# A graph network on one core: 24 instead of 20 of 98 receiver blocks summed by gathered rows, with their products placed in both kinds of TensorE stretches

## The chip, the core and the metric

The kernel runs on one core of a Trainium2 chip. The metric is the device time of an execution in microseconds. The engines are TensorE (PE, with its weight loads as PEld), VectorE (DVE), ScalarE (ACT), GpSimd (POOL) and SyncE (SP); SP and ACT issue plain transfers, POOL issues those that gather rows by a list of indices.

## The reference, cut to what matters

There are 12500 nodes with 64 features and 212500 directed edges, sorted by receiver (`dst`). Three layers take, for each node, the mean of its neighbours' rows; the last part takes the mean of the edges' own features and runs a small MLP.

```python
def _sage_conv(x, src, dst, Wl, Wr, b, n_nodes):
    msgs = x[src]
    summed = segment_sum(msgs, dst, num_segments=n_nodes)
    cnt = segment_sum(ones, dst, num_segments=n_nodes)
    agg = summed / maximum(cnt, 1.0)[:, None]
    return agg @ Wl + x @ Wr + b
...
h = maximum(_layernorm(x), 0.0)
x = x + L0(h)             # three _sage_conv, relu after the first two
h = maximum(_layernorm(x), 0.0)
x = x + L1(h)             # scatter_mean of edge_attr_64 by receiver,
                          # concatenated with h; 128 -> 64 -> 64 -> 64
```

## The kernel before, in words

The nodes are cut into 98 blocks of 128 (NB). A layer's neighbour sums are made per block of receivers, in one of two ways.

**Dense.** For 78 of the blocks (those from GB = 20 on), taken four at a time as 20 dense groups (the last has two), layer 0 builds the matrix of edge counts between all senders and the four receiver blocks, as 8-bit numbers. It is the product of two one-hot lists: DVE writes the lists (`hots`, L790 to L792), TensorE multiplies them (`pb`, L809), ACT writes the result to the matrix `m` (L812), and SP stores it in DRAM as `mat`. Layers 1 and 2 load it from there as `t`. A layer's sums are then products with the layer's rows, which are stored as three bf16 parts whose sum is the f32 value. `Layer.group` runs them in two kinds of steps: a **whole** step (L392) multiplies two parts of a sender block, 128 columns of weights, with the 512 receivers of the group; a **half** step (L403) multiplies the third part, 64 columns of weights, and steps of even and odd blocks use the lower and the upper half of the array. A group has 98 whole and 98 half steps.

**By edge.** For the first 20 blocks (GB), the rows of the edges' senders are fetched by an indirect transfer of POOL (`got`, L461), 128 edges at a time, EK = 19 times per block. DVE writes the matching one-hot of receivers (`own`, L336), and one product per 128 edges (`pg`, L489: 128x128 weights, 192 columns) adds them up. Per layer that is 20 x 19 = 380 fetches and products. A ring of NGOT = 8 buffers holds the fetched rows; the fetch for product i + 8 is issued behind product i (`Layer.use`). Every four blocks, `sums` transposes the result (L507), and `turn` (L425) and `mix` (L436, L440) follow, as they do for a dense group.

**The order** is written by hand. `Weave` runs a group in four stretches: 56 whole steps (TURN), 56 half steps, 42 whole, 42 half. Other work is hung on positions: `wide` on a count of whole steps over the layer (w), `narrow` on the index of a half step. The products by edge hang on `wide`, spread evenly by `spread` and `spot`; pb work hangs on both, 40 pairs of a four-block group on wide positions and 12 on narrow ones, two pairs at a time. The order holds for TensorE, DVE, ACT and POOL in layer 0, for TensorE and POOL in layer 1, for TensorE in layer 2.

**Lists.** For each node group, `index` finds where its edges begin: it fetches a tile of `dst` (`ends`, two buffers), lets ACT count in it (`inside`), and fetches the edges of single nodes (`to`, `of`). For blocks by edge, `lists` then fetches the edges' receivers and senders (`l_to`, `l_of`, L567) with POOL's indirect transfers, 8 per four blocks in two lots at steps 108 and 120 of the group's work, and DVE makes `place` and `rows_of` of them at step 150 (`places`).

**The edges' own features** are summed in layer 2, for all 98 blocks: SP loads a start address into a register (L1028) and then a block's edges from there (`raw`, `e_to`); 19 products per block (`pe`, L1138) stand among whole steps.

Of the kernel before, what the change touches and what calls it, by code (L numbers as in the profile page):

```python
# [11 lines left out]
F32 = mybir.dt.float32  # L12
# [17 lines left out]
P = 128  # L30
D = 64
# [12 lines left out]
WD = 5  # L44
FAR = 1 << 23
EK = 19
GB = 20
H1 = 10
QE = 5

# [21 lines left out]
def in_order(  # L72
# [221 lines left out]
    class Weave:  # L294
# [2 lines left out]

        def __init__(self):
            self.w, self.seq, self.wides, self.narrows = 0, 0, [], []

        def wide(self, pos, fn):
            self.seq += 1
            heapq.heappush(self.wides, (pos, self.seq, fn))

        def narrow(self, pos, sub, fn):
            self.seq += 1
# [2 lines left out]
        def run(self, whole, half):  # L309


            half = enumerate(half)
            for n in (TURN, None):
                for _ in islice(whole, n):
                    self.w += 1
                    while self.wides and self.wides[0][0] <= self.w:
                        heapq.heappop(self.wides)[2]()
                for i, _ in islice(half, n):
                    due = [f for f in self.narrows if f[0] <= i and f[1] <= self.w]
                    for f in sorted(due):  # L320
                        self.narrows.remove(f)
                        f[3]()
                    heapq.heapify(self.narrows)

        def rest(self):
            while self.wides or self.narrows:
                while self.narrows:
                    heapq.heappop(self.narrows)[3]()
                if self.wides:
                    heapq.heappop(self.wides)[2]()  # L330
# [13 lines left out]
    HALVES = ((0, H1), (H1, EK))  # L344
    CUTS = [(k, min(k + QE, EK)) for k in range(0, EK, QE)]
    NC = len(CUTS)
    NGOT = 8

    psd = ctx.enter_context(tc.tile_pool(name="ps_dense", bufs=1, space=PSUM))
    psc = ctx.enter_context(tc.tile_pool(name="ps_conv", bufs=1, space=PSUM))  # L350
# [5 lines left out]
    class Layer:  # L356
# [18 lines left out]
        def hand_over(self, to):  # L375

            w = self.weave
            for pos, _, f in sorted(w.wides, key=lambda a: a[:2]):
                to.weave.wide(pos - w.w, f)
            for sub, pos, _, f in sorted(w.narrows, key=lambda a: a[:3]):  # L380
                to.weave.narrow(pos - w.w, sub, f)
            self.weave, self.gap = to.weave, 0
# [96 lines left out]
        def use(self, i):  # L479
# [20 lines left out]
            if b % 4 == 3:  # L500
# [14 lines left out]
                w.narrow(w.w + 1, 40, sums)  # L515
                w.narrow(w.w + 1, 68, own_rows)

    steps = NB * len(dense_groups)

    def spot(i, first):  # L520
# [2 lines left out]

    def spread(layer, first):
        for i in range(EK * GB):
            layer.weave.wide(spot(i, first), lambda i=i: layer.use(i))


    TW = 4 * P
# [14 lines left out]
    with ExitStack() as s:  # L544
# [27 lines left out]
        def index(j, box):  # L572


            n0 = node0[:, j : j + 1]
            at = begins[:, j : j + 1]
            own = 32 * min(4, NB - 4 * j)
            tile = lambda name, n, dtype=F32, bufs=2: idx.tile([P, n], dtype, name=name, bufs=bufs)

            def over(t, bias, n, dtype, name, to):  # L580

                nc.scalar.activation(
                    tile(name, TW, dtype, 1)[:, :n], t, AF.Sign, bias=bias, scale=1.0, accum_out=to
                )

            def tiles():
                box["s"] = tile("tile_s", 1)
                over(heads, before[:, j : j + 1], TT, I8, "signs", box["s"])

            def ends():  # L590

                box["tile"] = tile("tile_of", 1)
                nc.vector.tensor_scalar(
                    box["tile"], box["s"], -0.5, 1.0 - TT / 2, op0=ALU.mult, op1=ALU.max
                )
                tile_i = tile("tile_i", 1, I32)
                nc.vector.tensor_scalar(tile_i, box["tile"], TT / 2 - 1.0, None, op0=ALU.add)
                box["ends"] = tile("ends", TW, I32)
                gather(box["ends"], tiles_d, tile_i[:, :1])

            def inside():
                box["in"] = tile("in_tile", 1)
                over(box["ends"], before[:, j : j + 1], TW, I8, "signs", box["in"])

            def edges():
                s = box["in"]
                nc.vector.tensor_scalar(
                    s, s, -0.5, TW / 2 + TW * (TT / 2 - 1.0), op0=ALU.mult, op1=ALU.add
                )
                nc.vector.scalar_tensor_tensor(  # L610
                    at, box["tile"], float(TW), s, op0=ALU.mult, op1=ALU.add
                )
                at_i = tile("at_i", 1, I32)
                nc.vector.tensor_scalar(at_i, at, float(EP - P), None, op0=ALU.min)
                box["to"], box["of"] = tile("to", P, I32), tile("of", P, I32)
                gather(box["to"], dst, at_i[:, :1])
                gather(box["of"], src, at_i[:, :1])

            def places():

                box["pos"], box["code"] = tile("pos", P), tile("code", P)
                pos, code = box["pos"], box["code"]
                nc.vector.tensor_scalar(pos, box["to"], n0, 7.0, op0=ALU.subtract, op1=ALU.min)
                nc.vector.scalar_tensor_tensor(
                    code, pos, float(1 << 14), box["of"], op0=ALU.mult, op1=ALU.add
                )
                behind = tile("junk", P, bufs=1)
                nc.vector.scalar_tensor_tensor(
                    behind, pos, size[:, :1], far, op0=ALU.is_ge, op1=ALU.mult
                )  # L630
                nc.vector.tensor_tensor(code, code, behind, op=ALU.max)

            def counts(d):
                if d == 0:
                    box["have"] = tile("have", WD + 1)
                over(
                    box["pos"], halves[:, d : d + 1], P, I8, "signs", box["have"][:, d : d + 1]
                )

            def alike():  # L640
                code = box["code"]
                for k in range(1, 5):
                    nc.vector.scalar_tensor_tensor(
                        tile("junk", P, bufs=1)[:own, k:], code[:own, k:], 0.0,
                        code[:own, : P - k], op0=ALU.add, op1=ALU.is_equal,
                        accum_out=twins[:own, j, k - 1 : k],
                    )
                have = tile("twice", WD)
                nc.vector.tensor_tensor(
                    have, box["have"][:, :WD], box["have"][:, 1:], op=ALU.subtract  # L650
                )
                box["by4"] = idx.tile([P, WD, 4], BF16, name="by4", bufs=2)
                nc.vector.tensor_tensor(
                    box["by4"], have[:, :, None].to_broadcast([P, WD, 4]),
                    mask4[:, None, :].to_broadcast([P, WD, 4]), op=ALU.mult,
                )
                box["first"] = tile("first", 4)
                nc.vector.tensor_scalar(box["first"], start4, at, None, op0=ALU.mult)

            return (  # L660
                [(0, tiles), (7, ends), (29, inside), (36, edges), (64, places)]
                + [(74 + 2 * d, lambda d=d: counts(d)) for d in range(WD + 1)]
                + [(91, alike)]
            )
# [67 lines left out]
        def lists(j):  # L732
# [3 lines left out]
            def edges(k0):  # L736
                if k0 == 0:
                    box["of"] = idx.tile([P, 4, EK], I32, name="l_of")
                    box["to"] = idx.tile([P, 4, EK], I32, name="l_to")
                for k in (k0, k0 + 1):  # L740
                    b = 4 * j + k
                    gather(box["to"][:, k, :], dst, mine[:, b : b + 1])
                    gather(box["of"][:, k, :], src, mine[:, b : b + 1])

            def places():
                for k in range(4):
# [273 lines left out]
    def load(b):  # L1020
        if b is None:
            return

        n = EK * P
        raw = ed.tile([P, n // P * D + 1], F32, name="raw")
        first = raw[:1, n // P * D :].bitcast(I32)
        nc.vector.tensor_scalar(first, mine[:1, b : b + 1], float(EP - n), None, op0=ALU.min)
        at0 = nc.values_load(  # L1028
            first, engines=[SP], min_val=0, max_val=EP - n,
            skip_runtime_bounds_check_because="it is clamped, and is not under 0",  # L1030
        )
        raw = raw[:, : n // P * D].rearrange("p (k d) -> p k d", d=D)
        nc.sync.dma_start(raw, edge[ds(at0, n), :].rearrange("(p k) d -> p k d", k=EK))
        if b < GB:
            box[b] = raw, place[:, b]
            return
        to = ed.tile([P, EK], I32, name="e_to")
        nc.sync.dma_start(to, dst[ds(at0, n), :].rearrange("(p k) o -> p (k o)", k=EK))
        at = ed.tile([P, EK, 2], BF16, name="e_at")
        nc.vector.tensor_scalar(  # L1040
            at, to[:, :, None].to_broadcast([P, EK, 2]), float(b * P), None, op0=ALU.subtract
# [736 lines left out]
```

## Time and profile before

| what | value |
|---|---|
| time, median of 3 runs | 2892.62 us (2887.84 to 2893.87) |
| the profiled execution | 2895.6 us, of which the span is 2893.7 |
| granted TensorE clock, mean | 0.985 |
| layer 0 with its preparation, about | 0 to 1130 us |
| layer 1, about | 1130 to 1876 us |
| layer 2 and the MLP, about | 1876 to 2894 us |
| TensorE busy in 160 to 1130, 1130 to 1876, 1876 to 2894 us | 948, 735, 997 us |
| POOL busy in the same stretches | 576, 363, 425 us |
| whole steps L392, halves L403, products by edge L489 | 5880, 5880, 1140 |

A line of the timeline gives the start and the length in us from the span's start, the engine (PE is a matmul), the line in the code, what is written and read, the tile of the array (128*64 is half of its columns), the shape and the count of merged instructions. Matmuls overlap, so the cost of one is read from the start of one row to the start of the next on the same engine, not from its length. A line of the waits gives who waited for whom, the total in us, the number of times and the longest. In the rows a matmul's outputs p1 and p2 are both called `p`.

### The profile page before, as it was taken

The numbers are of one execution on the slowest core, as the hardware profiler recorded it, in microseconds if no ns is written. First come the engines' busy times: TensorE is split into PE (matmuls) and PEld (weight loads), VectorE is DVE, ScalarE is ACT, GpSimd is POOL, SyncE is SP. The second block draws the span as 40 slices with busy tenths as digits, with TensorE's granted clock in tenths as the row PEclk, the third lists the DMA queues.
The fourth block names the chain that finished last, engine by engine and source line by source line (L and its number), as shares of the span: only waits on it lengthen the run. The fifth ranks groups of instructions, "written<-read, shape, count | busy, mean of one in ns | idle before, by whom it ended". The sixth has DMA issues, their size and how long they took to land.

```text
span 2893.7 us, 50078 instructions
## 1 busy us (share of the span) xinstructions
PE 2749.0 (95%) x19505; PEld 1600.9 (55%) x19505; DVE 1630.9 (56%) x3376; ACT 1122.5 (39%) x2339; POOL 1429.8 (49%) x1313
## 2 busy tenths in 40 slices
PE   1699999999999998999999999999999999999997
PEld 0455555555555554555555555655656565565655
DVE  8878788788788771211111111166666566666663
ACT  4666566666666661100000000033333333434332
POOL 5345667667575640555555555244444344444440
PEclk9999999999999998999999999999999999999998
DMA  3334434444444346766656665577667676667661
GB/s 97 160 128 169 154 137 169 169 164 149 160 167 156 138 158 224 236 212 210 208 190 205 210 212 191 191 232 238 218 200 226 195 231 216 203 219 232 207 211 36
DMA packets 203194, 537.43 MB, mean 186 GB/s; under 512 B 83874, under 2 KB 92195, under 8 KB 197955
## 3 DMA queue, kind: packets, MB, share of 16 engines
q1 hardware_dynamic: 143890, 458.08, 44.2%
q0 software_dynamic: 41360, 66.33, 10.2%
q10 hardware_dynamic: 17696, 9.74, 1.1%
q8 instruction: 154, 2.52, 0.4%
q14 instruction: 94, 0.76, 0.1%
HBM read 391.11 MB, written 142.90 MB: 185 GB/s over the span
## 4 chain that ended last, share of the span: by engine, by line
PE 83%; DVE 12%; DMA 3%; issue 1%; ACT 1%; POOL 0%; SPq 0%; ACTq 0%; DVEq 0%; POOLq 0%
PE p L392 39%; PE p L403 21%; PE pb L809 6%; PE pe L1138 5%; PE pg L489 3%; DVE c L792 3%; PE po L436 3%; PE po L440 3%; DVE h L790 2%; PE pt L425 2%; DVE h L791 1%; PE pm L1177 1%; PE pm L1186 1%; DMA ends<-in_dst_dram,tile_i 1%; DMA e_to<-in_dst_dram 1%
## 5 line engine op out<-in xcount | busy, mean ns | idle before, releaser
L461 POOL DMA_INDIRECT got<-h_d,rows_of x1140 | 1244.2, 1091 | 1246.0 <-PE pg L489 881.0
L812 ACT CAST m<-pb 128x490 uint16<-128x490 f32 (+1 forms) x1014 | 545.7, 564 | 329.1 <-PE pb L809 318.4
L392 PE MATMUL p<-m,rows 128*128 128x512 fp8e3 (+1 forms) x1960 | 569.6, 378 | 0.8 <-ACT m L812 0.8
L392 PEld LDWEIGHTS <-rows 128*128 128x128 bf16 x3920 | 374.6, 100 | 245.6 <-issue 45.9
L392 PE MATMUL p<-t,rows 128*128 128x512 fp8e3 (+1 forms) x1960 | 491.8, 378 | 0.9 <-ACT rows L263 0.9
L392 PE MATMUL p<-t,m 128*128 128x512 fp8e3 (+1 forms) x1960 | 458.4, 376 | 0.0
L809 PE MATMUL pb<-c,h 128*128 128x245 bf16 x2028 | 371.2, 276 | 57.0 <-ACT m L812 42.0
L336 DVE TENSOR_TENSOR own<-iota_l,place 128x640 bf16<-128x640 bf16 (+3 forms) x280 | 144.2, 516 | 360.2 <-PE pg L489 337.0
L403 PEld LDWEIGHTS <-rows 128*64 128x64 bf16 x3920 | 224.9, 110 | 217.5 <-issue 79.1
L809 PEld LDWEIGHTS <-h 128*128 128x128 bf16 x2028 | 190.9, 99 | 263.4 <-issue 105.5
L792 DVE TENSOR_TENSOR c<-iota_c,col 128x1968 bf16<-128x1968 bf16 (+1 forms) x234 | 298.6, 1276 | 0.0
L489 PE MATMUL pg<-got,own 128*128 128x192 bf16 x1140 | 281.7, 247 | 15.7 <-DVE ga L496 8.3
L392 PEld LDWEIGHTS <-m 128*128 128x128 bf16 x1960 | 184.7, 99 | 184.0 <-issue 13.9
L403 PE MATMUL p<-m,rows 128*64 128x512 fp8e3 (+1 forms) x1960 | 254.1, 378 | 0.0
L403 PE MATMUL p<-t,rows 128*64 128x512 fp8e3 (+1 forms) x1960 | 252.0, 377 | 0.0
L1052 ACT CAST cut<-raw 128x640 bf16<-128x640 f32 x196 | 136.5, 697 | 247.7 <-PE pe L1138 221.6
L790 DVE TENSOR_TENSOR h<-iota_l,lo 128x1024 bf16<-128x1024 bf16 (+1 forms) x234 | 173.6, 742 | 94.9 <-PE pb L809 94.4
L403 PE MATMUL p<-t,m 128*64 128x512 fp8e3 (+1 forms) x1960 | 225.5, 375 | 0.0
L1054 ACT CAST cut<-e_rest 128x640 bf16<-128x640 f32 x196 | 136.8, 698 | 221.5 <-DVE e_rest L1053 220.5
L1055 DVE TENSOR_TENSOR cut<-e_rest,cut 128x640 bf16<-128x640 f32 x196 | 154.8, 790 | 81.9 <-ACT cut L1054 81.4
L1138 PE MATMUL pe<-cut,own 128*128 128x192 bf16 x1862 | 188.3, 248 | 0.0
L1138 PEld LDWEIGHTS <-own 128*128 128x128 bf16 x1862 | 161.6, 99 | 40.5 <-issue 2.9
(189 smaller groups left out, 2566.1 us busy)
## 6 DMA issues: line engine op xcount, KB each, us to landing
t<-mat SPq DMA_DIRECT2D x546, 448.0 KB, 5.9
mat<-m SPq DMA_DIRECT2D x39, 3136.0 KB, 9.9
raw<-in_edge_dram SPq DMA_DIRECT2D x98, 608.0 KB, 4.1
got<-h_d,rows_of POOLq DMA_INDIRECT x1140
h_d<-rows SPq DMA_DIRECT2D x14, 336.0 KB, 2.2
h_d<-rows ACTq DMA_DIRECT2D x24, 192.0 KB, 2.5
h_d<-out SPq DMA_DIRECT2D x21, 192.0 KB, 1.9
m<-h_d SPq DMA_DIRECT2D x6, 576.0 KB
```

What stands on the lines that cost most here:

```text
L336: nc.vector.tensor_tensor(t[:, :n].rearrange("p k (c t) -> p k c t", t=2), iota_l.rearrange("p (c t) -> p c t", t=2)[:, None].to_broadcast ...
L392: nc.tensor.matmul(p1, rows[:, i, : 2 * D], at(i), start=i == 0, stop=i == NB - 1)
L403: nc.tensor.matmul(p2[h], rows[:, i, 2 * D :], at(i), start=i < 2, stop=i >= NB - 2)
L461: nc.gpsimd.indirect_dma_start(out=t, out_offset=None, in_=h_rows[self.l], in_offset=bass.IndirectOffsetOnAxis(ap=rows_of[:, b, k : k + 1] ...
L489: nc.tensor.matmul(self.pg[:, b % 2, :], self.owned.pop(i), self.fetched.pop(i), start=k == 0, stop=k == EK - 1,)
L790: nc.vector.tensor_tensor(split(th), pairs(iota_l, P), own(lo, P), op=ALU.is_equal)
L792: nc.vector.tensor_tensor(split(tc_), pairs(iota_c, CW), own(col, CW), op=ALU.is_equal)
L809: nc.tensor.matmul(pb[:, i, : HP * WD], h, c, start=True, stop=True)
L812: nc.scalar.copy(m[:, block // 2, :, o : o + 2 * k].rearrange("p h (w d) -> p h w d", d=k), pb[:, :, : HP * WD].rearrange("p w (h d) -> p ...
L1054: nc.scalar.copy(c[:, :, D : 2 * D], rest)
L1055: nc.vector.tensor_tensor(c[:, :, 2 * D :], rest, c[:, :, D : 2 * D], op=ALU.subtract)
L1138: nc.tensor.matmul(box["pe"], o[:, k - k0, :], c[:, k - k0, :], start=k == 0, stop=k == EK - 1)
```

## The change

GB becomes 24, NGOT 10. So four more blocks are summed by edge, 456 fetches and products per layer, and 19 dense groups are left. The products by edge are no longer hung on whole steps but on `even`, a count of slots: a whole step is one slot, and so is every second half step. A position of `spot` is multiplied by 1.5 to make it a slot. Layer 0's lists are loaded by SP, with an address from a register, as the edges of layer 2 are. The tile `ends` has one buffer where it had two. The loads of layer 2 use the same two helpers as the lists and are otherwise as before.

```diff
-GB = 20
+GB = 24
...
+        def even(self, pos, fn):
+
+            self.seq += 1
+            heapq.heappush(self.evens, (pos * 1.5, self.seq, fn))
+
+        def step(self, n):
+            self.slots += n
+            while self.evens and self.evens[0][0] <= self.slots:
+                heapq.heappop(self.evens)[2]()
...
                 for _ in islice(whole, n):
                     self.w += 1
+                    self.step(1)
                     while self.wides and self.wides[0][0] <= self.w:
                         heapq.heappop(self.wides)[2]()
                 for i, _ in islice(half, n):
+                    if i % 2:
+                        self.step(1)
                     due = [f for f in self.narrows if f[0] <= i and f[1] <= self.w]
...
-    NGOT = 8
+    NGOT = 10
...
+    def first_of(at):
+        return nc.values_load(
+            at, engines=[SP], min_val=0, max_val=EP - EK * P,
+            skip_runtime_bounds_check_because="it is clamped, and is not under 0",
+        )
+
+    def in_block(table, at0):
+        return table[ds(at0, EK * P), :].rearrange("(p k) d -> p (k d)", k=EK)
...
     def spread(layer, first):
         for i in range(EK * GB):
-            layer.weave.wide(spot(i, first), lambda i=i: layer.use(i))
+            layer.weave.even(spot(i, first), lambda i=i: layer.use(i))
...
-                box["ends"] = tile("ends", TW, I32)
+                box["ends"] = tile("ends", TW, I32, 1)
...
+                    box["at"] = idx.tile([1, 4], I32, name="l_at", bufs=2)
+                    nc.vector.tensor_scalar(
+                        box["at"], mine[:1, 4 * j : 4 * j + 4], float(EP - EK * P), None,
+                        op0=ALU.min,
+                    )
                 for k in (k0, k0 + 1):
-                    b = 4 * j + k
-                    gather(box["to"][:, k, :], dst, mine[:, b : b + 1])
-                    gather(box["of"][:, k, :], src, mine[:, b : b + 1])
+                    at0 = first_of(box["at"][:, k : k + 1])
+                    for to, ends in ((box["to"], dst), (box["of"], src)):
+                        nc.sync.dma_start(to[:, k, :], in_block(ends, at0))
```

More of the change, by code (lines that the diff above doesn't have):

```diff
@@ L299, in __init__ @@
             self.w, self.seq, self.wides, self.narrows = 0, 0, [], []
+            self.slots, self.evens = 0, []
         def wide(self, pos, fn):
@@ L325, in rest @@
         def rest(self):
+            assert not self.evens
             while self.wides or self.narrows:
@@ L377, in hand_over @@
             w = self.weave
+            assert not w.evens
             for pos, _, f in sorted(w.wides, key=lambda a: a[:2]):
@@ L1022, in load @@
             return
[L1024 to L1033, printed above, removed]
+        raw = ed.tile([P, EK * D + 1], F32, name="raw")
+        first = raw[:1, EK * D :].bitcast(I32)
+        nc.vector.tensor_scalar(first, mine[:1, b : b + 1], float(EP - EK * P), None, op0=ALU.min)
+        at0 = first_of(first)
+        nc.sync.dma_start(raw[:, : EK * D], in_block(edge, at0))
+        raw = raw[:, : EK * D].rearrange("p (k d) -> p k d", d=D)
         if b < GB:
@@ L1037, in load @@
         to = ed.tile([P, EK], I32, name="e_to")
-        nc.sync.dma_start(to, dst[ds(at0, n), :].rearrange("(p k) o -> p (k o)", k=EK))
+        nc.sync.dma_start(to, in_block(dst, at0))
         at = ed.tile([P, EK, 2], BF16, name="e_at")
```

## The prediction, made before the changed kernel was run

> **What bounds the kernel now.** I read the page's first and fourth part, then the timeline of TensorE in layer 0 and layer 1, then the waits of TensorE.
>
> ```profile
> PE 2749.0 (95%) x19505; PEld 1600.9 (55%) x19505; DVE 1630.9 (56%) x3376; ACT 1122.5 (39%) x2339; POOL 1429.8 (49%) x1313
> ...
> PE 83%; DVE 12%; DMA 3%; issue 1%; ACT 1%; POOL 0%; SPq 0%; ACTq 0%; DVEq 0%; POOLq 0%
> ```
>
> TensorE is busy for 95% of the span and holds 83% of the chain that ended last; no other engine comes near. So the forecast is a count of TensorE's own time, from start to start, because the durations (378 ns for a matmul whose successor starts after 216 ns) overlap. The timeline of TensorE in layer 0, around the end of a half stretch:
>
> ```profile
> 595.63 0.60 PE L809 MATMUL pb<-c,h 128*128 128x245 bf16 x4
> 596.16 1.70 PE L403 MATMUL p<-m,rows 128*64 128x512 fp8e3 x14
> 597.79 0.60 PE L809 MATMUL pb<-c,h 128*128 128x245 bf16 x4
> 598.32 1.05 PE L403 MATMUL p<-m,rows 128*64 128x512 fp8e3 x7
> 599.30 0.61 PE L392 MATMUL p<-m,rows 128*128 128x512 fp8e3 x2
> 599.75 0.38 PE L809 MATMUL pb<-c,h 128*128 128x245 bf16 x2
> 599.96 0.38 PE L392 MATMUL p<-m,rows 128*128 128x512 fp8e3 x1
> ```
>
> And in layer 1:
>
> ```profile
> 1411.60 0.25 PE L489 MATMUL pg<-got,own 128*128 128x192 bf16 x1
> 1411.68 1.03 PE L392 MATMUL p<-t,m 128*128 128x512 fp8e3 x4
> ...
> 1419.30 0.25 PE L489 MATMUL pg<-got,own 128*128 128x192 bf16 x1
> 1419.48 1.70 PE L403 MATMUL p<-t,m 128*64 128x512 fp8e3 x13
> ...
> 1421.68 4.72 PE L403 MATMUL p<-t,m 128*64 128x512 fp8e3 x42
> 1426.33 1.04 PE L392 MATMUL p<-t,m 128*128 128x512 fp8e3 x4
> ```
>
> What is to be seen, start to start:
> - Halves (L403) run two at a time. 42 take 4.65 us up to the next instruction, 14 take 1.63: 28 more cost 3.02, so a pair costs 0.2157. Seven take 0.98, as much as eight would: a half without a partner costs a pair's time, 0.108 more.
> - Leaving halves costs extra. 14 halves are 7 x 0.2157 = 1.51 but take 1.63: 0.12. Coming back: the four pb matmuls take 0.53 where two among whole steps take 0.21, so 0.10 more. The gather's matmul shows this way back too: 0.08 before a whole step (1411.60), 0.18 before a half (1419.30). So **each full-width visit inside a half stretch costs 0.22 us beside the work itself**. Among whole steps (L392, 0.2157 each) a gather's product costs only its 0.082.
>
> In the kernel before, all 1140 products of gathers stand among whole steps; in half stretches only pb, the f32 transposes of `sums` and fc make such visits.
>
> **The change, part by part.** The changed kernel's compiled order of TensorE shows what is placed where: 1368 gather products, of which 440 (148, 147 and 145 per layer) stand inside half stretches, each alone between two runs of halves.
>
> *Removed, on TensorE.* One dense group of four blocks in each of three layers: 98 whole x 0.2157 = 21.1; 49 pairs x 0.2157 = 10.6; the edges of its two half stretches 2 x 0.22 = 0.4. 32.1 x 3 = 96.4. In layer 0 also its building: 104 pb x 0.107 = 11.1 and six visits x 0.22 = 1.3. Together **-108.8 us**. Mix and turn of the four blocks stay (25 groups per layer either way).
>
> *Added, on TensorE.* 4 x 19 x 3 = 228 products x 0.082 = 18.7. 440 visits x 0.22 = 96.8. The order has 410 lone halves where it had 180: visits of gathers come after a complete pair by index, pb visits in the middle of one, so in layer 0 each now leaves a lone half for the other (80 to 222), and fc does so in layer 2; 230 x 0.108 = 24.8. For the sixth receiver group 4 f32 transposes per layer, 12 x 0.22 = 2.6, and 3 visits, 0.7. Together **+143.6**. Sum of TensorE: **+34.8**.
>
> The skill speaks to the disputed term. "TensorEngine Tiling (Array Packing)", Key Properties, says that changing the tiling mode drains TensorE, without a price; "TensorE: Matmul & The Clock Gate", Step-by-step, puts a drain at about 128 cycles, 53 ns at the 2.4 GHz used there. Two per visit are 0.107 us (an estimate from that page): 440 x 0.107 = 47, and the sum would be -15, faster. The trace has 0.22 for the visit and +35. The rows are of this kernel, with the same weights' shape (128x128) between the same halves, so they are used.
>
> *DVE.* It loses 12 building batches (L790 to L792: 0.742 + 0.74 + 1.276, some 33 us) and gains 48 `own` (0.5 each) and 12 reductions. All beside TensorE; it is 80% busy in layer 0, so this only takes pressure off.
>
> *POOL.* It gains 228 gathers (0.94 + 0.30 between them, 1.24 at best, about 1.5 in layer 0) and loses 40 list fetches (1.0 + 0.3). Cover: POOL idles 881 us waiting for products to free a buffer. With the even spread a gather is wanted every 5.53 slots in layer 1: 5.53 x 0.2157 + 0.08 = 1.27 us among whole steps, 1.49 in halves, against 1.24; with ten buffers it holds, by a small margin. Before, they were wanted every 4.7 whole steps (1.09 us) and made up for it in the halves. In layer 0 I expect one per 1.7 us against 1.4 to 1.5. The gain of evenness is bounded by these waits of layer 0:
>
> ```profile
> PE pg L489 <- DVE ga L496: 5.1, 4, 2.0
> PE pg L489 <- DVE own L336: 3.1, 1, 3.1
> PE pg L489 <- DMA got<-h_d,rows_of: 3.1, 2, 1.6
> ...
> PE pg L489 <- DVE tile_of L593: 1.2, 1, 1.2
> ```
>
> 12.5 us in all, and 3 in layer 2: between -15 and 0; I take -8.
>
> *`ends` with one buffer.* Three times in POOL's order after gathers began, the next `ends` fetch comes before ACT has read the last one; it then waits, at most 22 steps of some 0.33 us, 7 us (up to about 15 if a half stretch lies between), and the gathers queue behind it. Ten buffers at 1.7 us, less some 4 us from issue to landing, cover 13. Between 0 and +25; I take +2.
>
> *Lists on SP.* Per block a register load (0.27 us where the edge loads have one) and two issues of 0.33, then some 4.0 us to landing, as for e_to. The second half of a list is issued at step 120 and read by DVE (`places`) at 150, 10 us later or more; it needs about 6. SP's queue holds stores of mat and h_d ahead of it, which wait for ACT and DVE, and the stores behind it wait for the register load's DVE instruction. If it is late, DVE stands still and the building batches with it: bound +5 x 6 = 30 above, and below -5, since DVE already waited 7.3 us for POOL's lists; I take +1.
>
> Sum: 34.8 - 8 + 2 + 1 = **+30**. The profiled execution took 2895.6 us (span 2893.7 and 1.9 around it), 3 above the median; it would become 2925.6, the median 2892.6 becomes **2923**.
>
> **The rivals.**
> 1. *Visits are cheap* (the faster side). Place: the 440 gaps in half stretches. If the gather's weights could be loaded under the last pair, a visit would cost less than pb's. The sum is zero at (108.8 - 18.7 - 24.8 - 3.3) / 440 = 0.14 us per visit; at the skill's 0.107 it gives 2876, at nothing 2824. For it: nothing before shows a gather entered from a half. Against it: pb, whole steps and transposes are all entered 0.1 late, and the way back is shown for the gather itself. 9%.
> 2. *POOL or the lists fall behind.* In layer 1 POOL has 2% to spare among whole steps; if transfers push its 1.24 to 1.6, over the 1.45 that are on average available (some 735 us x 0.90 of the steps / 456), 456 x 0.15 = 68 us are lost in that layer; a smaller slip, or DVE held by lists and `ends`, gives 2935 to 2975. For it: gathers took up to 2.0 us beside a busy DVE. Against: in layer 1 they were steady. 15%.
> 3. *Layer 0 was held by DVE more than TensorE's waits show* (12% of the chain), and with one group less to build its 30 us of waits go: 2893, no change. 6%.
> 4. My sum holds, 2908 to 2938: 70%.
>
> **How the numbers follow.** The time is case 4's. The range takes in case 3's end below and the nearer half of case 2 above: 2894 to 2950. What this measurement can tell from no change is about 0.2%, 6 us. Faster by more: 9% (case 1). Same: 5%. Slower: 86%.
>
> **What would show it.** Right: the halves' timeline broken by single L489 every 5 or 6 pairs, about 0.30 us from the gather's predecessor pair to the next beyond the pair's own time; layer 1 longer by some 7 to 8 us although it has 19 groups; TensorE's waits about as short as before. Wrong: a visit at 0.14 or less; TensorE waiting for got or own by tens of us in layer 1 (case 2); layer 0 shorter while layers 1 and 2 grow (case 3).

## The result and the profile after

The changed kernel takes 2941.4 us (2940.8 to 2942.8) where the kernel before takes 2892.6: a ratio of 1.017 (95% interval 1.0155 to 1.019), +48.8 us. The forecast was +30, inside the range.

The page of the changed kernel, parts 1 and 4:

```profile
PE 2781.7 (95%) x19052; PEld 1544.9 (53%) x19052; DVE 1613.4 (55%) x3398; ACT 1094.6 (37%) x2287; POOL 1614.7 (55%) x1501
...
PE 84%; DVE 9%; DMA 2%; issue 2%; ACT 1%; POOL 1%; ACTq 0%; SPq 0%; POOLq 0%; DVEq 0%
```

TensorE runs 453 matmuls fewer and is busy 32.7 us longer (2749.0 to 2781.7). The span grew by 45.8 (2893.7 to 2939.5), so the other 13.1 are time in which TensorE stood idle. TensorE still holds the chain; POOL rose by 185 us of busy time and holds 1% of it.

Where the time went, from the busy time of each engine in three stretches cut at the last half step of each layer. The columns: stretch, its length, TensorE busy, PEld, DVE, ACT, POOL, then granted clock, DMA share and GB/s. Before:

```profile
116.00:1129.00 1013.00, 984.19 (x7030) 570.51 (x7030) 786.76 (x1625) 631.28 (x1425) 583.57 (x485) 0.99 0.44 158
1129.00:1877.00 748.00, 737.05 (x5027) 403.91 (x5023) 110.93 (x253) 53.09 (x106) 363.06 (x380) 0.99 0.64 208
1877.00:2864.00 987.00, 979.03 (x7224) 595.42 (x7224) 624.34 (x1249) 372.86 (x653) 425.12 (x380) 0.99 0.67 211
```

And the changed kernel:

```profile
116.00:1150.00 1034.00, 996.86 (x6808) 553.49 (x6807) 761.09 (x1612) 602.82 (x1372) 616.23 (x521) 0.99 0.43 152
1150.00:1911.00 761.00, 748.83 (x4901) 381.13 (x4899) 118.82 (x272) 53.09 (x106) 438.82 (x456) 0.98 0.62 201
1911.00:2908.00 997.00, 985.66 (x7125) 577.73 (x7119) 624.76 (x1264) 373.22 (x653) 500.06 (x456) 0.99 0.64 206
```

Each layer has one group less and takes longer: +21, +13 and +10 us. In layer 1 nearly all of it is busy time (+11.8), at a clock of 0.98 for 0.99; in layer 0 it is 12.7 busy and 8.3 idle.

The timeline of TensorE in a half stretch of layer 1, now:

```profile
1299.32 1.49 PE L419 MATMUL p<-t,m 128*64 128x512 fp8e3 x12
1300.73 0.26 PE L505 MATMUL pg<-got,own 128*128 128x192 bf16 x1
1300.92 1.27 PE L419 MATMUL p<-t,m 128*64 128x512 fp8e3 x10
```

L419 is the half step, L505 the gather's product. Twelve halves are six pairs, 1.29 us at 0.2157 each; they take 1.41 up to the product: 0.12. From the product to the next half is 0.19 where the product itself needs 0.08: 0.11. The visit costs 0.22 to 0.23 beside the product, as forecast from pb. Over the 99 such visits of layer 1 that stand between two even runs of halves at full clock, the median is 0.228.

The waits of TensorE in layer 0 (160 to 1150 us) of the changed kernel:

```profile
PE pb L840 <- ACT m L843: 9.8, 9, 4.1
PE pg L505 <- DVE ga L512: 9.2, 7, 2.4
PE pg L505 <- DMA got<-h_d,rows_of: 4.1, 3, 2.2
PE pt L523 <- DVE tile_of L619: 2.2, 1, 2.2
PE pg L505 <- DVE own L351: 2.1, 1, 2.1
PE po L452 <- DVE e L425: 2.1, 3, 0.9
```

With 0.7 more they are 30.2 us; the seven rows of before are 22.2. Of these the prediction does not show:

```profile
PE po L436 <- DVE e L409: 7.8, 12, 1.9
PE pb L809 <- ACT m L812: 1.6, 2, 1.3
```

The products wait about as much as before (15.4 for 12.5). The largest growth is pb's wait for ACT (1.6 to 9.8), which the prediction does not name; what makes it is open. POOL's own waits show `ends` holding POOL twice for 20 us after the gathers had begun (20.3 us before the fetch at 377 us, behind ACT; 20.1 before the one at 836 us, where the profile names DVE's `h`, but ACT's read of `ends` had ended only 0.3 us before), longer than the 7 to 15 worked out. The ten buffers covered most of it: products waited 4.1 us for fetched rows.

### The profile page after: what moved, and what is told of

Read it like the earlier page. It is cut to its first block, busy times and chain, and to the rows that moved or that the text cites. A ratio compares the mean times of both kernels' runs of the same rounds, so it can differ in the third digit from the quotient of the medians.

```text
span 2939.5 us, 49694 instructions
## 1 busy us (share of the span) xinstructions
PE 2781.7 (95%) x19052; PEld 1544.9 (53%) x19052; DVE 1613.4 (55%) x3398; ACT 1094.6 (37%) x2287; POOL 1614.7 (55%) x1501
## 4 chain that ended last, share of the span: by engine, by line
PE 84%; DVE 9%; DMA 2%; issue 2%; ACT 1%; POOL 1%; ACTq 0%; SPq 0%; POOLq 0%; DVEq 0%
PE p L408 36%; PE p L419 23%; PE pb L840 6%; PE pg L505 5%; PE pe L1164 5%; PE po L456 3%; PE po L452 2%; DVE c L823 2%; PE pm L1203 2%; PE pt L441 1%; DVE h L821 1%; DMA ends<-in_dst_dram,tile_i 1%; DVE h L822 1%; PE pm L1212 1%; POOL got L477 1%
## 5 line engine op out<-in xcount | busy, mean ns | idle before, releaser
L477 POOL DMA_INDIRECT got<-h_d,rows_of x1368 | 1477.8, 1080 | 1073.8 <-PE pg L505 745.9
L843 ACT CAST m<-pb 128x490 uint16<-128x490 f32 (+1 forms) x962 | 516.6, 565 | 361.0 <-PE pb L840 350.5
L408 PE MATMUL p<-m,rows 128*128 128x512 fp8e3 (+1 forms) x1862 | 539.8, 379 | 0.8 <-ACT m L843 0.8
L408 PE MATMUL p<-t,rows 128*128 128x512 fp8e3 (+1 forms) x1862 | 463.6, 377 | 0.1
L408 PE MATMUL p<-t,m 128*128 128x512 fp8e3 (+1 forms) x1862 | 433.1, 378 | 0.0
L351 DVE TENSOR_TENSOR own<-iota_l,place 128x640 bf16<-128x640 bf16 (+2 forms) x336 | 172.1, 514 | 449.9 <-PE pg L505 436.6
L505 PE MATMUL pg<-got,own 128*128 128x192 bf16 x1368 | 342.6, 250 | 19.9 <-DVE ga L512 12.6
L419 PEld LDWEIGHTS <-rows 128*64 128x64 bf16 x3724 | 199.5, 109 | 195.0 <-issue 79.0
L419 PE MATMUL p<-m,rows 128*64 128x512 fp8e3 (+1 forms) x1862 | 285.9, 384 | 0.0
L505 PEld LDWEIGHTS <-own 128*128 128x128 bf16 x1368 | 133.1, 97 | 271.2 <-issue 174.2
L419 PE MATMUL p<-t,rows 128*64 128x512 fp8e3 (+1 forms) x1862 | 261.6, 379 | 0.0
L419 PE MATMUL p<-t,m 128*64 128x512 fp8e3 (+1 forms) x1862 | 243.2, 379 | 0.0
```

Source lines behind the costliest of these rows:

```text
L351: nc.vector.tensor_tensor(t[:, :n].rearrange("p k (c t) -> p k c t", t=2), iota_l.rearrange("p (c t) -> p c t", t=2)[:, None].to_broadcast ...
L408: nc.tensor.matmul(p1, rows[:, i, : 2 * D], at(i), start=i == 0, stop=i == NB - 1)
L419: nc.tensor.matmul(p2[h], rows[:, i, 2 * D :], at(i), start=i < 2, stop=i >= NB - 2)
L477: nc.gpsimd.indirect_dma_start(out=t, out_offset=None, in_=h_rows[self.l], in_offset=bass.IndirectOffsetOnAxis(ap=rows_of[:, b, k : k + 1] ...
L505: nc.tensor.matmul(self.pg[:, b % 2, :], self.owned.pop(i), self.fetched.pop(i), start=k == 0, stop=k == EK - 1,)
L843: nc.scalar.copy(m[:, block // 2, :, o : o + 2 * k].rearrange("p h (w d) -> p h w d", d=k), pb[:, :, : HP * WD].rearrange("p w (h d) -> p ...
```

## The experiments

These runs were made on three chips, where the kernel before took 2944 to 2970 us; beside the change it took 2893. Each ratio below is to the kernel before on the same chip; profiles are of one execution each, and where two from different chips are compared, the text says so.

**1. The placement alone.** The kernel before with the class's slot count and `spread` of the changed one, and nothing else:

```diff
-            layer.weave.wide(spot(i, first), lambda i=i: layer.use(i))
+            layer.weave.even(spot(i, first), lambda i=i: layer.use(i))
```

> The kernel before (20 blocks by edge, 8 buffers, lists on POOL) with only the placement changed: products hung on the slot count. No more gathers than before, so POOL has more time for each. Theory A (a full-width visit inside a half stretch costs TensorE 0.22 us, a lone half 0.108): 370 visits and 232 more lone halves, 81 + 25 = +104 us, about 2997. Rival B (visits are nearly free; the loss of the change comes from waits for POOL, ends and lists that 24 blocks bring): about 2893, within 10.

Measured: 3002.3 us, ratio 1.020 (1.0155 to 1.0245), +56. That is half of theory A's +104 and no support for rival B's nothing. The profile says where the other half is. Its span is 2997.8, 104 us over the profile of before that stands ahead of the prediction, but 53 over one from another chip where the kernel before is as slow as beside this run (experiment 5). Over the three stretches TensorE is busy 2799 us, 99 more than in the first profile of before (2700) and 78 more than in that of the slower chip (2721), and idle 53 us, for 48 and 77. In layer 1 it takes 775 us, and TensorE waits for nothing but the layer's start (10.5 us, 10.4 before), so the 28 us over the 747 of the first profile are visits: 124 of them in that layer at 0.22, 27. So the visits cost about what theory A counts, but on the slower chip the kernel before has gaps and short stalls of its own (there its layer 1 takes 774 us), which layer 1 of this run does not show.

**2. The count alone.** The changed kernel, 24 blocks, 10 buffers and lists by SP, with the products on whole steps as before (the diff of experiment 1 reversed).

> The changed kernel with its products hung on whole steps again, as before: 24 blocks, 10 buffers, lists on SP, no visit in half stretches. Theory A: TensorE's own time falls by 88 us against before, so 2805, plus what it waits for gathers, which are now wanted every 0.88 us in whole stretches against 1.24 of POOL: with 10 buffers and the halves to catch up 0 to 40 us, 2805 to 2845. Rival B (POOL sets the pace at 24 blocks, so the spread was needed): waits for got of over 100 us, 2900 or more.

Measured: 3078.9 us, ratio 1.048 (1.042 to 1.054). Theory A fell for the sum, in layers 0 and 1. But the waits are not rival B's either; in layer 1 (1194 to 2074 us) TensorE's longest are:

```profile
PE p L419 <- issue: 53.1, 74, 2.2
PE pt L441 <- issue: 12.3, 22, 1.1
PE po L452 <- DVE o L467: 10.5, 1, 10.5
PE pt L441 <- ACT gat L525: 9.7, 2, 5.0
```

No row of that layer, among those not shown either, says that it waited for a fetched row; 65 us are waits inside half stretches in which nothing that the profile shows was missing. The timeline of one:

```profile
1411.21 0.95 POOL L477 DMA_INDIRECT got<-h_d,rows_of  x1 [0.30 <-issue]
1412.14 0.77 PEld L441 LDWEIGHTS <-m 128*64 128x64 bf16 x10
1412.35 0.67 PE L441 MATMUL pt<-identb,m 128*64 128x128 bf16 x9
1412.99 0.94 POOL L477 DMA_INDIRECT got<-h_d,rows_of  x1 [0.83 <-remote]
1413.42 0.22 PE L441 MATMUL pt<-identb,m 128*64 128x128 bf16 x1 [0.40 <-issue]
1414.12 0.11 PEld L441 LDWEIGHTS <-m 128*64 128x64 bf16 x1 [1.21 <-issue]
1414.13 0.24 PE L441 MATMUL pt<-identb,m 128*64 128x128 bf16 x1 [0.49 <-issue]
...
1414.85 0.38 PE L419 MATMUL p<-t,m 128*64 128x512 fp8e3 x1 [0.30 <-issue]
1415.55 2.55 PEld L419 LDWEIGHTS <-m 128*64 128x64 bf16 x26 [1.23 <-issue]
```

Weight loads and matmuls stop together and go on a few at a time, at 1412.80 (the ninth transpose), 1413.42, 1414.13, 1414.85 and 1415.55: steps of 0.7 us. Besides, the granted clock of the two layers is 0.96 and 0.95. In layer 1 that is worth some 44 us (an estimate, 0.05 x 880), most of the 63 by which TensorE's busy time there (775 us) lies over the 712 counted. In layer 2 of the same run, where POOL has more time per product, there is next to none of this: 970 us against 988 and 990 in the two profiles of before, 18 to 20 less where the count says 25.

**3. The lists alone.** The changed kernel with GB = 20, NGOT = 8 and products on whole steps.

> The changed kernel with GB back at 20, 8 buffers and products on whole steps: against before only layer 0's lists by SP and the single ends buffer differ. Theory A: nothing measurable, within 6 us of before. Rival B (late lists or the wait for ends hold DVE or POOL): +10 to +30.

Measured: 2925.3 us, ratio 0.993 (0.990 to 0.996), -21. Both theories missed: the lists by SP (or the single `ends` buffer with them) are a gain on this chip. Layer 0 up to its last half step ends at 1131 us, at 1150 in the profile of before on a slower chip and at 1129 on the faster one, so a gain on the faster chip is not shown. That POOL, with 40 fetches less, is what this frees is likely, but only argued.

**4. The bursts.** In the changed kernel, all slots of a half stretch counted at its end:

```diff
-                    if i % 2:
-                        self.step(1)
+                    if i + 1 in (TURN, NB):
+                        self.step(TURN // 2 if i + 1 == TURN else (NB - TURN) // 2)
```

> The changed kernel with the slots of a half stretch counted all at its end: among whole steps the products keep the slot spacing (1.27 us in layer 1), and those that would have fallen into the halves follow as a burst of 4 or 5 at the edge to the next whole steps. No visit in half stretches. Theory A: 2805 in TensorE's own time as for products on whole steps, and fewer waits for POOL than there, so 2805 to 2830. Rival B (waits for POOL and lists made the loss): near the changed kernel's 2941.

Measured: 3126.2 us, ratio 1.062 (1.058 to 1.067), the worst of all, though no product stands in a half stretch. Both theories missed. TensorE's waits in halves with no releaser are 38.4 us in 62 times here, those for `ga` 31.2, those of pb for nothing shown 28.2, and the clock is 0.957. Visits aren't the only price that a placement has.

**5. Both kernels again**, for profiles on a slower chip.

> The kernel before, unchanged, for a profile on this chip. In the four runs above the kernel before took 2946 us, not 2893. Theory C (with the products among whole steps alone, the half stretches are at the mercy of something that differs between chips: TensorE shows gaps of about 0.7 us there that name no releaser, as in the profile of 24 blocks on whole steps): on a chip where it takes about 2946, such gaps sum to 30 to 60 us; where it takes 2893, none. Rival: the chip is slower everywhere, and all rows of the profile are longer by 1.8%.

> The changed kernel, unchanged. Theory C: its half stretches are broken by visits and have no such gaps, so it takes 2941 on any chip, and its ratio to the kernel before is 1.017 on a chip where that takes 2893 and about 1.00 where it takes 2946. Rival (a chip slower everywhere): ratio 1.017 on any chip, 2995 beside 2946.

Measured: before 2948.0 us (beside 2944.4); the changed kernel 2981.9, ratio 1.013 (1.009 to 1.018). Theory C fell in both halves: the changed kernel isn't spared (+40 on this chip, against +55 for the one before), and its ratio stays above 1. The rival that all rows grow fell as well: layer 2 takes 990 us in before (988 on the first chip); layers 0 and 1 carry all of it, 1034 and 774 for 1013 and 747. In layer 1 the kernel before now shows the gaps, which its first profile does not have:

```profile
PE po L436 <- DVE o L451: 10.1, 1, 10.1
PE p L403 <- issue: 6.4, 17, 0.8
PE pg L489 <- issue: 3.3, 3, 2.1
```

Not 30 to 60 us, but 10 in sum where waits are marked, with TensorE busy 749 us for 737. As a matmul lasts 378 ns while its successor starts after 216, a stall of up to some 160 ns does not show as idle; such short stalls and a slightly lower clock (0.98 for 0.99) are the likely rest. What differs between the chips is open.

**6. Lone halves.** The slot of a half stretch counted at even half steps (`if i % 2 == 0`), so that visits of pb and of gathers stand at one parity.

> The changed kernel with the slot of a half stretch counted at the even half step instead of the odd one. As many gathers and visits (459 for 440), but visits of pb and of gathers now stand at the same parity: 228 lone halves instead of 410. Theory A: 182 x 0.108 = 20 us less, and 18 visits fewer in all, 4 us: 24 under the changed kernel. Rival (lone halves cost nothing, they pair across a visit): the same as the changed kernel.

Measured: 2968.6 us, ratio 1.008 (1.005 to 1.011), 13 under the changed kernel on the same chip, where 24 were expected. But the profiles say that this is not theory A's saving at half its size. Up to its last half step, layer 0 takes 21 us less than in the profile of experiment 5 (1035 for 1056), and layers 1 and 2 take 8 and 9 us more (789 for 781, 1003 for 994). The edit moved the lone halves and did not do away with them: most half stretches now start and end with an odd run.

```profile
1305.91 1.05 PE L419 MATMUL p<-t,m 128*64 128x512 fp8e3 x7
1306.89 0.26 PE L505 MATMUL pg<-got,own 128*128 128x192 bf16 x1
```

Seven halves take 0.98 us, as much as eight. Counted in the two traces (runs of halves between full-width instructions, at full clock), layers 0, 1 and 2 have 68, 67 and 51 odd runs here for 173, 0 and 0, and in both kernels an odd run takes 0.104 us more than its number of halves alone would add. So the price of a lone half holds, and the counts in the expectation do not. The two profiled executions differ by 2 us only; the 13 between the medians are not explained.

**7. Fewer visits, as many products.** Slots released every 11 pairs; the core of the edit:

```diff
-                    if i % 2:
-                        self.step(1)
+                    if i % 2 and (i % 22 == 21 or i + 1 in (TURN, NB)):
+                        self.step(self.owed + 1)
+                        self.owed = 0
+                    elif i % 2:
+                        self.owed += 1
```

> The changed kernel with its products in half stretches gathered up: slots are released only every 11 pairs and at the ends of a stretch, so 197 visits of two or three products instead of 440 of one, as many gathers. Theory A (the price is per visit, not per product): 243 visits fewer and 62 lone halves fewer, 59 us under the changed kernel, about 2883, less if POOL is late with a burst. Rival B (the price is for the product or for gathers as such): the same as the changed kernel. Theory C adds the chip's gaps in the longer unbroken runs of 22 halves.

Measured: 2970.8 us, ratio 1.009 (1.006 to 1.012), 11 under the changed kernel, not 59. TensorE's busy time in the three stretches fell by 31 us (1009, 758 and 983 to 993, 753 and 973), although its mean clock fell from 0.978 to 0.971, which is worth some 21 us (an estimate, 0.007 x 2980). Without that, busy time would be about 50 us less, near theory A's 59. Idle time in the stretches rose from 81 to 116 us. So fewer visits do save TensorE's work, and stalls and the lower clock give most of it back.

**8. Who makes the gaps.** The kernel of experiment 2, with every second gather of layer 1 left out; its product reads the rows of the one before. The core of the edit:

```diff
+            if self.l == 1 and i % 2:
+                self.fetched[i] = self.fetched.get(i - 1, self.recent)
+                return
```

> 24 blocks with products on whole steps, but in layer 1 only every second gather is fetched; the product after it reads the same rows again, so layer 1 adds up wrong rows. TensorE's order and number of instructions stay as with all gathers, where layer 1 took 880 us (712 in TensorE's own time). If POOL's gathers (their bursts in the half stretches, or their lateness) bring the gaps of 0.7 us there: layer 1 takes 720 to 750, about 2930 in all. If TensorE's own instruction stream does (more instructions per microsecond than it is fed with): layer 1 stays within 30 us of 880.

Measured: 2955.1 us in all, ratio 0.995 (0.993 to 0.997). Layer 1 takes 731 us where it took 880 (on another chip), and TensorE's order is the same there. Its waits from 1200 to 2050 us:

```profile
PE po L452 <- DVE o L467: 10.2, 1, 10.2
PE p L419 <- issue: 3.7, 6, 1.0
```

The gaps are gone (53.1 and 12.3 to 3.7). So TensorE's order of instructions doesn't bring them by itself; the gathers have a part in it. Half the gathers also means half their traffic and half the waits of POOL, so which of these acts is not told apart. The same run's layers 0 and 2 kept all gathers; layer 0 stays long (1098 us up to its last half step, 1078 in experiment 2), so the other chip is not what freed layer 1. Layer 2 takes 978.

**9. 24 blocks where POOL has time.** 20 blocks in layers 0 and 1, 24 in layer 2 alone, on whole steps, lists by SP; the core of the edit:

```diff
+            self.gb = GL if l == NL - 1 else GB        # GB = 20, GL = 24
...
-            for g, (j0, n) in enumerate(dense_groups):
+            for g, (j0, n) in last_groups:             # those from block GL on
                 layer.group(columns(g), j0, n)
```

> 20 blocks by edge in layers 0 and 1, 24 in layer 2 alone (its dense groups start one later; the lists of the four blocks are loaded as well), products on whole steps, lists by SP. Theory A: layer 2 gains the 24 us of TensorE that the count says (it was 18 to 20 shorter with 24 blocks on whole steps), as POOL has time there; the rest as with 20 blocks and lists by SP, which took 21 us less than before beside it. About 40 under before, ratio 0.986. Rival (what 24 blocks gain is lost in layer 2 as well, to gaps or waits): 0.993, as 20 blocks with lists by SP.

Measured: 2923.4 us beside 2970.3, ratio 0.986 (0.982 to 0.989). It is faster than the kernel before, and the changed one was slower in every comparison. The sum came as expected, its parts did not: in the profile layer 2 takes 976 us, 11 to 14 under the two profiles of before (both from other chips) and not 24, so the larger part of the 47 us would be layers 0 and 1 with the lists by SP.

## Why the prediction was right, and where its sizes were off

- *TensorE is the bound, and its time can be counted from start to start*: right. +34.8 was counted; its busy time grew by 32.7. That these are so close is in part luck: the lone halves were counted 10 to 14 us too high, visits cost some 3.5 us more than at 0.22, and the sum leaves out the clock, whose records in the trace hold 75 us at half clock in the three stretches for 65 before, some 5 us of work. Its two sides show apart: a group less saves 18 to 20 us in layer 2 (experiment 2), visits alone cost 28 in layer 1 (experiment 1).
- *0.22 us per visit, from pb*: right; the gather's own rows show 0.228 at the median, in the changed kernel on both chips and in experiment 1. The drain of 53 ns of the Trainium skill's "TensorE: Matmul & The Clock Gate" (Step-by-step), taken twice, is the prediction's estimate that would have made the change a gain of 15; the measurement decides against it.
- *Lone halves, 0.108 each*: the price is right (0.104 in the traces), the number is not. Layer 0 has 178 odd runs for 73 before, layers 1 and 2 have none between full-width instructions; with the runs beside transposes and fc, which can be counted in more than one way, 105 to 145 more than before and not 230. That is 11 to 15 us, not 24.8.
- *Layer 1 longer by 7 to 8 us*: it was 13.9, from the last half step of layer 0 to that of layer 1 (747.3 to 761.2). The wait at its start is 1.3 us longer (11.7 for 10.4), 147 visits at 0.228 add 1.2, and 27 us at half clock for 20 are worth some 3.
- *-8 for evenness, +2 for `ends`, +1 for lists*: this is the term that was mis-sized. -5 in all were forecast, TensorE's idle time grew by 13. The products' waits in layer 0 did not shrink (12.5 to 15.4): 9.2 of them are for DVE's `ga`, which an even spread of POOL's fetches does not touch, and pb's wait for ACT, put at nothing, grew by 8. `ends` held POOL for 20 us twice, more than the 15 allowed, though products then waited only 4.1 us for rows. The lists by SP did no harm that shows, and were a gain on a slower chip (experiment 3).
- *Rival 1, cheap visits*: fell. (With 50 and 97 us taken off 2923, its figures would be 2873 and 2826, not 2876 and 2824.) *Rival 3, layer 0 gains 30*: fell, it lost 21.
- *Rival 2, POOL behind in layer 1*: not for the changed kernel. But what I wrote under POOL, that products on whole steps "made up for it in the halves", misses what this costs once there are 24: catching up at one gather per 1.25 us beside half stretches comes with TensorE's gaps, and with half the gathers they go (experiment 8). So the spread of the change has a use that the prediction did not price: with 24 blocks it is worse without it (1.048 against 1.013, on chips where before takes about 2945). The two together still lose, since the visits cost about what the groups save.

## What to carry to other kernels

Price each placement by starts: a full-width matmul dropped into a run of half-width ones costs its time plus 0.22 us here, and this change would have broken even at about 0.12 (0.228 less 48.8 / 440, an estimate; the prediction's sum said 0.14). But gathering the visits into bursts gave most of that back in waits and clock, so the price to compare is the whole stage's time. Before moving work to an idle engine, ask when that engine does it: on whole steps, 24 blocks by edge gain where POOL keeps pace (layer 2) and lose where it catches up in bursts. Compare with the old kernel on the same chip, always; here it differs by 2 to 3% between chips, more than the effects of most of these edits.

## What the runs showed of the hardware that was not expected

- Half stretches can be cut into steps of about 0.7 us in which neither weight loads nor matmuls start and no releaser shows. They were most with POOL's gathers back to back and all products on whole steps, and went with half the gathers (53.1 + 12.3 us to 3.7 in layer 1). The changed kernel shows none in its first profile and a few on the slower chip (3.5 us before half steps in experiment 5). What in the chip makes them is open: the gathers' traffic, their issue back to back and the supply of TensorE's instructions are not told apart.
- The mean granted clock was lower where such stalls were many: 0.985 in the first profile of before, 0.966 with 24 blocks on whole steps, 0.957 with bursts; in layer 1 0.95, and 0.98 once half the gathers were gone.
- The price of a visit did not differ between chips: 0.228 us at the median in layer 1 of the changed kernel on the first chip and on the slower one, and in experiment 1, although the kernel before took 53 us more on the slower ones.
